# Two half-steps of a fused attention loop trade places

## The chip, the cores and the metric

The kernel runs on one core of a Trainium2 chip. The time is that of the whole launch on the device, in microseconds; lower is better. The core has a matrix engine (TensorE, shown as PE, its weight loads as PEld), a vector engine (VectorE, DVE), an engine for activation functions (ScalarE, ACT), a general engine (GpSimd, POOL), and queues that start DMA transfers. The engines run side by side and meet at semaphores. TensorE writes to PSUM, eight banks of 128 x 512 floats, from which VectorE and ScalarE read.

## What is computed

Two layers over an input of 2 images, 256 channels, 64 x 64 positions, all in fp32. The first layer is attention with 8 heads of 32 channels over 4096 positions, with a projection and a residual. The second is a non-local block (pooled keys and values, softmax over 1024 keys, a 1x1 convolution, batch normalization, residual). Nearly all time goes to the first:

```python
qkv = jnp.einsum('oc,bchw->bohw', w_qkv, x)
q, k, v = jnp.split(qkv, 3, axis=1)
...
scores = jnp.einsum('bhdi,bhdj->bhij', q, k) / jnp.sqrt(jnp.asarray(d, x.dtype))
attn = jax.nn.softmax(scores, axis=-1)
out = jnp.einsum('bhij,bhdj->bhdi', attn, v)
out = out.reshape(b, c, h, w)
return jnp.einsum('oc,bchw->bohw', w_proj, out) + x
```

## The kernel before

**Blocks and steps.** The attention of one image, one group of four heads (a quad) and 512 queries is a block: 2 images x 2 quads x 8 groups of queries make 32 blocks. A block (the class at L389, the loops at L529 to L569 in `attend`) takes its 4096 keys in 32 steps of 128; `j` counts them. A step needs, for each of the four heads, the scores of 128 keys against 512 queries (`score`, L404), their exponential (L551, two heads at a time, on ScalarE), and the sum of values weighted with them (`weigh`, L435), which is added to the running numerator `num` on VectorE (L450). The weighted sum of a step is issued one step later.

**Row groups.** A head has 32 channels, so a score matmul fills 32 of TensorE's 128 rows, and head h lies on rows 32h to 32h + 31. Matmuls on different rows can run at the same time. The weighted sum uses all 128 rows and 32 columns for each head.

**Maxima beside it.** The softmax subtracts the true maximum of each row. The maxima of a block are found a block earlier, in a second pass over the same scores, laid out with the queries on the partitions. That pass is a generator, `maxima` (L346), which `advance(maxes)` moves on by one half-step. Each half-step issues two products (`product`, L261), for two heads. So a step of the main loop has two slots, and in each the two score matmuls of one pair of heads stand beside two products of the other pair: four row groups in use.

**Plain and pair.** Heads 0 and 1 take their maxima plainly: each product of 512 keys goes to a VectorE reduce (`plain`, L273, the reduce at L276). Heads 2 and 3 take pairs of key chunks (`pair`, L278): a product with the difference of two chunks, whose relu ScalarE takes (L283), and in the next half-step of that head the product with the first chunk, to which VectorE adds the relu while it reduces (`joint`, L288; two instructions at L290). The two heads are a half-step apart, so each half-step of heads 2, 3 has one relu and one joint, the relu head first. In the first block of a new quad half of their work is plain too (L330). In the order before, the half-step of heads 2, 3 comes first in a step (L353), beside the scores of heads 0, 1 (L538), and that of heads 0, 1 second, beside the scores of heads 2, 3.

**The scores' banks.** Two tiles of two banks each hold the scores (`scores`, L68), one for each pair of heads, for four steps at a time. At `j % 4 == 0` the tile is started with the negative maxima (`subtract`, L424, two short matmuls; there the products are issued ahead of the scores), and in the next three steps the products with key differences are added to what stands there, so a score matmul waits for the exponential of the same pair one step before.

**The scratch banks.** The other four banks are one rotating pool, `ps_m` (L66, `scratch`, L71). The four products of a step, the weighted sum, and now and then a projection of q, k or v (`make`, L168), the row terms (`rows`, L147) or the denominator (L486) take a bank from it, in the order of issue; a new tile waits for whatever reads the tile that had the bank.

**Sums of the exponentials.** For the denominator, GpSimd adds the exponentials of heads 0, 1 into one tile (L469), and those of heads 2, 3 are added two steps at a time by accumulating DMA transfers, started from GpSimd's queue (L477) into two tiles that are added by one more such transfer (L483). The exponentials of heads 0, 1 lie in single tiles (six of them, L76), those of heads 2, 3 in double tiles for two steps (five, L79), which come free when their transfer has landed.

**Order.** Each engine runs its instructions in the order in which this code issues them, except that `issue_after` keeps an exponential behind the last relu issued (L549), and a few others behind named instructions. A step is: slot one, slot two, the weighted sum of the step before, the additions (`add`, L458), the pieces of normalization and projection that are due.

Of the kernel before, what the change touches and what calls it, by code (L numbers as in the profile page):

```python
# [35 lines left out]
def conv_attention(  # L36
# [31 lines left out]
    def scores(name):  # L68
        return ps_s.tile([P, 2, NB], F32, tag="s", name=name)
# [6 lines left out]
    def single(name):  # L76
        return probs.tile([P, 2, NB], F32, tag="one", name=name, bufs=ONES)

    def double(name):  # L79
        return probs.tile([P, 2, 2, NB], F32, tag="two", name=name, bufs=TWOS)  # L80
# [56 lines left out]
    def negate(name, neg):  # L137


        rest = work.tile([P, NB // P, QH], F32, tag="rest", name=f"rest_{name}")  # L140
        nc.gpsimd.tensor_copy(t[:, :, :, 0], neg)
        nc.gpsimd.tensor_sub(rest, neg, t[:, :, :, 0])
        nc.gpsimd.tensor_copy(t[:, :, :, 1], rest)
        nc.gpsimd.tensor_sub(rest, rest, t[:, :, :, 1])
        nc.gpsimd.tensor_copy(t[:, :, :, 2], rest)

        def rows():  # L147
            pt = scratch(f"pt_{name}")
            for j in range(NB // P):
                nc.tensor.matmul(  # L150
                    pt[:, bass.ts(j, P)],
                    t[:, j].rearrange("p h d -> p (h d)"),
                    ident_b,
                    start=True,
                    stop=True,
                )
            to = work.tile([P, NB], BF16, tag="rows", name=f"rows_{name}")
            nc.scalar.copy(to, pt)
            return to

        return rows
# [77 lines left out]
    def between(n, half):  # L239
        two = k[n][:, N // 2 * half + NB :]  # L240
        nc.gpsimd.tensor_sub(mid_kd[:, half, :], two[:, NB : 2 * NB], two[:, :NB])
# [3 lines left out]
    def during(n, i):  # L245
        if i < NI - 2:
            return [("q", n, i + 2), ("k", n + 1, i), ("v", n + 1, i)]
        if i == NI - 2:
            return [("k", n + 1, i), ("k", n + 1, i + 1), ("q", n + 1, 0)]
        return [("v", n + 1, i - 1), ("v", n + 1, i), ("q", n + 1, 1)]  # L250
# [50 lines left out]
    def first_block():  # L301


        for jp in range(NI // 2):
            for g in range(G):
                over = double(f"over_{jp}_{g}").rearrange("p a b n -> p (a b) n")
                for what in range(2):
                    if what == 0:
                        keys = (kd[0] if jp < NI // 4 else last_kd)[:, jp % (NI // 4), :]
                    else:  # L310
                        keys = k[0][:, bass.ts(2 * jp, NB)]
                    s = scores(f"ps_{jp}_{g}_{what}")
                    ps = [
                        product(0, 0, g, h, keys, s[:, h - 2, :] if h >= 2 else None)
                        for h in range(QH)
                    ]
                    for h in range(QH):
                        if what == 0:
                            nc.scalar.activation(over[:, h, :], ps[h], AF.Relu)
                        else:  # L320
                            joint(ps[h], over[:, h, :], g, h, jp)
                    yield
# [3 lines left out]
    def of_head(n, i, h):  # L326

        chunks = 0 if h < 2 else NI // 2 if i == 0 and n > 0 else NI  # L330
        pairs = [(g, jp) for jp in range(chunks // 2) for g in range(G)]
        plains = [(g, j) for g in range(G) for j in range(chunks, NI)]
        if h == 3:
            if not plains:
                g, jp = pairs.pop()
                plains = [(g, 2 * jp), (g, 2 * jp + 1)]
            plain(n, i, plains[0][0], h, plains[0][1])
            plains = plains[1:]
            yield
        for x in pairs:  # L340
            yield from pair(n, i, x[0], h, x[1])
        for x in plains:
            plain(n, i, x[0], h, x[1])
            yield

    def maxima(n, i):  # L346
        if (n, i) == (0, 0):
            yield from first_block()
        else:
            heads = [of_head(n, i, h) for h in range(QH)]  # L350
            for step in range(G * NI):

                for two in ((2, 3) if step % 2 == 0 else (3, 2)), (0, 1):  # L353
                    for h in two:
                        next(heads[h])
                    yield
        neg = work.tile([P, NB // P, QH], F32, tag="neg", name=f"neg_{n}_{i}")
        nc.vector.tensor_reduce(neg, part, AX.X, ALU.max, negate=True)
        rows.append(negate(f"{n}_{i}", neg))
        if i == 0 and n > 0:  # L360
            nc.vector.memset(part[:, :, 2:, :], LEAST)
# [11 lines left out]
    def advance(steps, n=1):  # L373
        for _ in range(n):
            next(steps, None)
# [12 lines left out]
    def attend(b, y):  # L388
# [15 lines left out]
        def score(s, pair, blk, j):  # L404

            half, c, cols = j // 16, j % 4, bass.ts(j % 16 // 4, P)
            if c == 0:
                kj = k[blk.n][:, bass.ts(keys(j), P)]
            elif c == 2:
                kj = mid_kd[:, half, cols]  # L410
            else:
                kj = (last_kd if half else kd[blk.n])[:, c // 2, cols]
            for t in range(2):
                h = 2 * pair + t
                nc.tensor.matmul(  # L415
                    s[:, t, :],
                    kj[bass.ts(h, D), :],
                    q[blk.n, blk.i][bass.ts(h, D), :],
                    start=False,
                    stop=True,  # L420
                    skip_group_check=j % 4 > 0,
                )

        def subtract(s, pair, blk):  # L424
            for t in range(2):
                h = 2 * pair + t
                nc.tensor.matmul(  # L427
                    s[:, t, :],
                    ones_b[bass.ts(h, D), :],
                    rows[blk.rows][bass.ts(h, D), :],  # L430
                    start=True,
                    stop=False,
                )
# [95 lines left out]
        for qd in range(QUADS):  # L529
            for i in range(NI):  # L530
                blk = Block(qd, i)
                items = [x for x in during(blk.n, i) if x[1] < len(QUAD)]
                both = [None, None]
                for j in range(NJ):
                    if j % 2 == 0:
                        two = double(f"p_{blk.name}_{j}_1")
                    p = [single(f"p_{blk.name}_{j}_0"), two[:, j % 2]]
                    for pair in range(2):  # L538
                        if j % 4 == 0:
                            s = both[pair] = scores(f"s_{blk.name}_{j}_{pair}")  # L540
                            subtract(s, pair, blk)
                            advance(maxes)
                            score(s, pair, blk, j)
                        else:
                            s = both[pair]
                            score(s, pair, blk, j)
                            advance(maxes)
                        with ExitStack() as order:
                            if cut is not None:  # L549
                                order.enter_context(tc.issue_after(cut.ins))  # L550
                            nc.scalar.activation(p[pair], s, AF.Exp, scale=scale)  # L551
                    if waiting is not None:
                        weigh(*waiting)
                        if j == 0:
                            normal = normalize(waiting[0])
                    add(blk, j, p, two)
                    waiting = blk, j, p
                    if j == 2 or j >= AFTER:
                        advance(normal)
                    if j % 2 == 0:  # L560
                        make_rows()
                        if (i, j) == (0, 2) and blk.n > 0:
                            between(blk.n, 1)
                        if (i, j) == (0, NJ // 4) and blk.n > 0:
                            differences(blk.n, 1, last_kd)
                        if (i, j) == (NI - 1, NJ // 2 + 2) and blk.n + 1 < len(QUAD):
                            between(blk.n + 1, 0)
                    elif j % 8 == 3 and j > 8 and items:
                        advance(make(*items.pop(0)), 9)  # L569
# [289 lines left out]
```

## Time and profile before

| | us |
|---|---|
| median of three runs | 4026.8 (4026.47 to 4027.5) |
| the profiled execution | 4027.6 |
| its span, first to last instruction | 4025.5 |
| until the first weighted sum | 103.5 |
| one block (630.00 to 735.65) | 105.65 |
| of it VectorE / ScalarE / GpSimd busy | 84.0 / 80.5 / 85.6 |
| projection and non-local layer, first image | about 292 |
| granted TensorE clock, mean | 0.997 |

The attention blocks take about 3.3 of the 4.0 ms, so what matters is the length of one step, 2.99 or 3.09 us, repeated some 600 times without anything else in it. TensorE shows busy throughout. Its records overlap: four matmuls on four row groups are in flight together, and an fp32 matmul is two passes, each with a record. On TensorE's timeline a step therefore shows as a row of starts 0.43 us apart, and its length is read from one weighted sum (L439) to the next. The timeline's columns are the start, the time covered by the group in us, the engine, line, operation and tiles, and in brackets the idle time before it with what ended it.

### The profile page before, as it was taken

To read this page: it belongs to the slowest core of one execution; us is meant where nothing else is said; L and a number is where in the kernel's file an instruction comes from. 1 tells how busy PE (TensorE), PEld (TensorE's weight loads), DVE (VectorE), ACT (ScalarE), POOL (GpSimd) and SP (SyncE) were. 2 spreads that over 40 slices of the span, in tenths; PEclk is the share of its full clock that TensorE was granted. 3 is DMA by queue.
4 is the path that set the end of the run, shared out by engine and by line. 5 is a ranking of instruction groups with operands and counts; after the bars stand their busy time and mean duration, and the time that the engine had idled before them with its cause. 6 is when DMAs were issued, how large, how long until landed. Compare 5 with 4: busy or idle time off the path is not lost.

```text
span 4025.5 us, 72980 instructions
## 1 busy us (share of the span) xinstructions
PE 3993.3 (99%) x28592; PEld 1460.0 (36%) x28592; DVE 2959.7 (74%) x5451; ACT 2668.1 (66%) x3328; POOL 2898.1 (72%) x1851
## 2 busy tenths in 40 slices
PE   9999999999999999999999999999999999999998
PEld 4333333333333333333333333333333333333333
DVE  5877777788777887774457877777888888884444
ACT  4777777777777777751137777777677777777121
POOL 1888888888888888871447888888888888886043
PEclk9999999999999999999999999999999999999999
DMA  1677777877777777880017787877788777778200
GB/s 56 141 163 159 161 165 162 168 162 165 159 161 163 161 161 162 169 199 12 21 35 163 163 167 164 167 161 167 161 167 166 162 162 163 162 161 184 72 16 26
DMA packets 113946, 569.60 MB, mean 141 GB/s; under 512 B 20296, under 2 KB 22600, under 8 KB 52416
## 3 DMA queue, kind: packets, MB, share of 16 engines
q0 software_dynamic: 68832, 501.25, 61.1%
q1 hardware_dynamic: 44080, 62.88, 5.3%
q8 instruction: 224, 3.67, 0.4%
q14 instruction: 122, 1.00, 0.1%
q10 hardware_dynamic: 688, 0.79, 0.1%
HBM read 54.78 MB, written 8.88 MB: 16 GB/s over the span
## 4 chain that ended last, share of the span: by engine, by line
PE 97%; DVE 2%; ACT 0%; POOL 0%; DMA 0%; issue 0%; DVEq 0%; ACTq 0%
PE ps L264 27%; PE w L439 25%; PE s L415 24%; PE y L715 5%; PE s L427 3%; PE v L186 2%; PE q L198 2%; PE k L198 2%; PE den L495 1%; PE proj L584 1%; PE g L640 1%; DVE r L729 1%; PE f L683 1%; PE f L749 1%; PE tp L624 0%; PE tp L620 0%
## 5 line engine op out<-in xcount | busy, mean ns | idle before, releaser
L469 POOL TENSOR_TENSOR p<-p,p 128x1024 f32<-128x1024 f32 x945 | 2293.6, 2427 | 569.9 <-ACT p L551 442.6
L264 PE MATMUL ps<-k,q 32*128 32x512 f32 x6232 | 2115.5, 619 | 2.4 <-DVE part L290 1.0
L551 ACT ACTIVATE p<-s 128x1024 f32<-128x1024 f32 x2048 | 1983.4, 1024 | 106.5 <-PE ps L264 61.2
L276 DVE TENSOR_REDUCE part<-ps 128x1 f32<-128x512 f32 x2136 | 1373.7, 686 | 87.9 <-PE ps L264 57.7
L290 DVE CUSTOM_DVE_ANT_0 ps<-ps,over 128x512 f32<-128x512 f32 x980 | 683.7, 700 | 572.3 <-PE ps L264 410.1
L439 PE MATMUL w<-p,v 128*32 128x512 f32 x8192 | 1092.7, 605 | 0.0
L283 ACT ACTIVATE over<-ps 128x512 f32<-128x512 f32 x916 | 547.2, 597 | 568.6 <-PE ps L264 552.0
L264 PEld LDWEIGHTS ps<-k,q 32*128 32x128 f32 x6232 | 809.7, 184 | 207.6 <-DVE part L276 48.6
L450 DVE TENSOR_TENSOR num<-num,w 128x512 f32<-128x512 f32 x992 | 670.7, 676 | 38.5 <-PE w L439 34.4
L264 PE MATMUL ps<-kd,q 32*128 32x512 f32 x1056 | 568.4, 643 | 1.0 <-POOL kd L219 0.7
L415 PE MATMUL s<-q,k 32*128 32x512 f32 x2048 | 514.6, 593 | 0.0
L415 PE MATMUL s<-q,last_kd 32*128 32x512 f32 x2048 | 510.1, 614 | 0.0
L415 PE MATMUL s<-q,kd 32*128 32x512 f32 x2048 | 509.9, 615 | 0.1
L415 PE MATMUL s<-q,mid_kd 32*128 32x512 f32 x2048 | 509.6, 615 | 0.0
L264 PE MATMUL ps<-last_kd,q 32*128 32x512 f32 x904 | 481.1, 639 | 1.5 <-POOL last_kd L219 1.5
L439 PEld LDWEIGHTS w<-p,v 128*32 128x32 f32 x8192 | 161.5, 108 | 777.4 <-ACT over L283 684.9
L477 POOL DMA_DIRECT2D p<-p x448 | 390.3, 871 | 66.0 <-ACT p L551 65.2
L415 PEld LDWEIGHTS s<-q,mid_kd 32*128 32x128 f32 x2048 | 173.5, 183 | 309.3 <-ACT p L551 306.8
L415 PEld LDWEIGHTS s<-q,kd 32*128 32x128 f32 x2048 | 174.2, 184 | 241.0 <-ACT p L551 215.1
L415 PEld LDWEIGHTS s<-q,last_kd 32*128 32x128 f32 x2048 | 173.5, 183 | 229.6 <-ACT p L551 213.0
L715 PE MATMUL y<-p,kv 128*128 128x512 f32 x512 | 240.0, 608 | 6.4 <-DVE r L729 6.4
L764 ACT ACTIVATE p<-f 128x1024 f32<-128x1024 f32 x64 | 65.5, 1024 | 248.5 <-PE f L749 219.2
(108 smaller groups left out, 2629.5 us busy)
## 6 DMA issues: line engine op xcount, KB each, us to landing
p<-p POOLq DMA_DIRECT2D x478, 1024.0 KB, 7.5
x_k<-in_x_dram SPq DMA_DIRECT2D x32, 512.0 KB
x_q<-in_x_dram SPq DMA_DIRECT2D x30, 512.0 KB
x_res<-in_x_dram SPq DMA_DIRECT2D x16, 512.0 KB
out_dram<-z SPq DMA_DIRECT2D x16, 512.0 KB
r<-flat SPq DMA_DIRECT2D x120, 64.0 KB
x_v<-in_x_dram SPq DMA_DIRECT2D x6, 512.0 KB
wqk_sb<-in_wqk_dram ACTq DMA_DIRECT2D x1, 512.0 KB
```

The source lines that it names most:

```text
L198: nc.tensor.matmul(pq, wqk_sb[:, c, qd, 0 if what == "q" else 1, :], xc[:, c, :], start=(c == 0), stop=(c == NC - 1),)
L264: nc.tensor.matmul(ps, q[n, i][bass.ts(h, D), bass.ts(g, P)], keys[bass.ts(h, D), :], start=True, stop=True,)
L276: reduced = nc.vector.tensor_reduce(part[:, g, h, j : j + 1], ps, AX.X, ALU.max)
L283: cut = nc.scalar.activation(over, ps, AF.Relu)
L290: reduced = nc.vector.tensor_tensor_reduce(out=ps, in0=ps, in1=over, scale=1.0, scalar=LEAST, op0=ALU.add, op1=ALU.max, accum_out=part[:, ...
L415: nc.tensor.matmul(s[:, t, :], kj[bass.ts(h, D), :], q[blk.n, blk.i][bass.ts(h, D), :], start=False, stop=True, skip_group_check=j % 4 > 0,)
L439: nc.tensor.matmul(w[bass.ts(h, D), :], v[blk.n][:, keys(j), h, :], p[h // 2][:, h % 2, :], start=True, stop=True,)
L450: nc.vector.tensor_add(blk.num, blk.num, w)
L469: added = nc.gpsimd.tensor_add(blk.sums[0], blk.sums[0], p[0])
L477: nc.gpsimd.dma_start(out=blk.sums[n], in_=two, accum_op=ALU.add)
L551: nc.scalar.activation(p[pair], s, AF.Exp, scale=scale)
L715: nc.tensor.matmul(acc[i][o], wg[:, 2 * t + j, bass.ts(o, P)], p[:, j, :], **edge)
```

## The change

The two slots of a step trade places: the scores of heads 2, 3 beside the plain products of heads 0, 1 come first, and the scores of heads 0, 1 beside the pair products of heads 2, 3 second. The weighted sum stays at the end of the step, and which scores stand beside which products stays too.

```diff
             for step in range(G * NI):
 
-                for two in ((2, 3) if step % 2 == 0 else (3, 2)), (0, 1):
+                for two in (0, 1), ((2, 3) if step % 2 == 0 else (3, 2)):
                     for h in two:
                         next(heads[h])
                     yield
...
                     p = [single(f"p_{blk.name}_{j}_0"), two[:, j % 2]]
-                    for pair in range(2):
+                    for pair in (1, 0):
                         if j % 4 == 0:
                             s = both[pair] = scores(f"s_{blk.name}_{j}_{pair}")
                             subtract(s, pair, blk)
```

## The prediction

> **What bounds the kernel now.** I read the page's busy shares first, then its chain, then the table of waits, and then the timeline of one stretch, since shares hide which wait ends last.
>
> ```profile
> PE 3993.3 (99%) x28592; PEld 1460.0 (36%) x28592; DVE 2959.7 (74%) x5451; ACT 2668.1 (66%) x3328; POOL 2898.1 (72%) x1851
> PE 97%; DVE 2%; ACT 0%; POOL 0%; DMA 0%; issue 0%; DVEq 0%; ACTq 0%
> ```
>
> TensorE is never empty, but a matmul counts as busy while it waits its turn in a row group, so 99% does not say that it runs at its own pace. The table of waits (total us, times, longest) shows who holds it:
>
> ```profile
> PEld s L415 <- ACT p L551: 735.0, 1104, 1.0
> PEld w L439 <- ACT over L283: 684.9, 903, 0.8
> ...
> PEld ps L264 <- DVE num L450: 41.8, 211, 0.4
> ```
>
> The two long rows are about 0.7 us each time, at every change between the scores' tiling and the weighted sum's tiling: the weight load waits for the array to empty, whatever engine is named. The third row is small, but it is the one that is late. TensorE's timeline (start, length, group):
>
> ```profile
> 1000.46 1.07 PE L439 MATMUL w<-p,v 128*32 128x512 f32 x8
> 1001.45 0.70 PE L415 MATMUL s<-q,last_kd 32*128 32x512 f32 x2
> ...
> 1002.84 0.59 PE L264 MATMUL ps<-k,q 32*128 32x512 f32 x1
> 1002.86 0.59 PE L415 MATMUL s<-q,last_kd 32*128 32x512 f32 x2
> 1002.93 0.59 PE L264 MATMUL ps<-k,q 32*128 32x512 f32 x1
> 1003.45 1.06 PE L439 MATMUL w<-p,v 128*32 128x512 f32 x8
> 1004.44 0.70 PE L415 MATMUL s<-q,mid_kd 32*128 32x512 f32 x2
> ...
> 1006.02 0.59 PE L264 MATMUL ps<-k,q 32*128 32x512 f32 x1
> 1006.53 1.07 PE L439 MATMUL w<-p,v 128*32 128x512 f32 x8
> 1007.53 0.70 PE L415 MATMUL s<-q,last_kd 32*128 32x512 f32 x2
> ```
>
> One step of 128 keys is first slot, second slot, weighted sum W. Step one lasts 1004.44 − 1001.45 = 2.99, the next 3.09. In the second one the last product stands alone at 1006.02, and W starts 0.52 later; in the first it is at 1002.93, some 0.06 behind its mates. The weight loads and VectorE say why:
>
> ```profile
> 1002.39 0.21 PEld L264 LDWEIGHTS ps<-k,q 32*128 32x128 f32 x2 [0.20 <-DVE num L450]
> ...
> 1005.48 0.29 PEld L264 LDWEIGHTS ps<-k,q 32*128 32x128 f32 x2
> ```
>
> ```profile
> 1002.82 0.70 DVE L290 CUSTOM_DVE_ANT_0 ps<-ps,over 128x512 f32<-128x512 f32 x1 [0.48 <-PE ps L264]
> 1003.44 0.14 DVE L290 DVE_READ_ACCUMULATOR2_ANT part<- 128x1 f32 x1
> 1003.55 1.29 DVE L276 TENSOR_REDUCE part<-ps 128x1 f32<-128x512 f32 x2
> 1004.75 0.68 DVE L450 TENSOR_TENSOR num<-num,w 128x512 f32<-128x512 f32 x1
> ```
>
> Per step five tiles go through four scratch banks in turn, so each waits for the tile four places earlier. Before, the order is relu head, joint head, plain, plain, W; the second plain product takes the bank of the last W, which the addition into num frees. That addition stands last in VectorE's queue, at 1004.75 to 1005.43; the load follows 0.05 later (1005.48). This closes a loop over two steps. From a first slot's start: joint +1.37, num ends +3.98, load +4.03, the late product's second pass +0.535 (1005.48 to 1006.02), W +0.52, next first slot +0.99: 6.08. Measured: 1007.53 − 1001.45 = 6.08.
>
> TensorE alone would need 0.96 (slot to slot) + 0.97 (second slot to W, its last pass on time) + 0.99 = 2.92 a step.
>
> **What the Trainium skill says.** "TensorE: Matmul & The Clock Gate", Part 3, The mechanism: matmuls in different row groups overlap, but start and end in program order. The trace agrees: four start within 0.02 us, and one late product holds W. "TensorEngine Tiling (Array Packing)", Key Properties: a change of tiling mode drains TensorE; the trace shows 0.99 from W's start to the next slot for two passes of 0.43. "PSUM — Partial Sum Buffer", Specifications: 8 banks of 2 KiB; here four hold the scores, four the scratch. The first page also calls ScalarE's and VectorE's queues strict FIFO (Part 1, Architectural detail), and in the timeline num never passes the reduces ahead of it.
>
> **The change part by part.** No instruction is added or removed. The order of the built program shows that the pairing stays (scores of heads 0, 1 beside products of heads 2, 3, and the reverse); only the place of W in the cycle moves. Let 0 be the start of the new first slot (plain products c, d), the pair products being a (relu) and b (joint).
>
> *Banks.* The order becomes c, d, a, b, W. So W waits for c's reduce of the same step, d for the relu a of the step before, b for the num addition. The waits in the built program name just these.
>
> *VectorE.* A slot's first results are complete 1.13 after its start, and an engine picks them up 0.08 later (relu 1002.67 after an end at 1002.59). c's reduce 1.21 to 1.90 (0.69); d 0.61 later, 1.82; joint 0.61 later, 2.43 (its data is there at 0.96 + 1.37 = 2.33); num 0.72 after the joint (1002.82 to about 1003.54), 3.15, since W's data comes at about 3.10; it ends at 3.83. Before it was 3.98: the joint no longer leads the queue with VectorE idle before it. Then load 3.88, second pass +0.535 = 4.41, W 4.93, next slot 5.92 for two steps, 0.16 less than 6.08.
>
> *New wait.* c's reduce ends at 1.90, release 0.05: W may start at 1.95, where TensorE alone gives 1.93. So a step is at least 1.95 + 0.99 = 2.95.
>
> *Sum.* Every fourth step has the row subtraction and is TensorE's own (3.13 between W starts; about 3.12 after). The three between take 2.99, 3.09, 2.985 = 9.06 before; after, 2.95, 5.92 − 2.95 = 2.97, 2.95 = 8.87. Over the block from 630.00 to 735.65 (105.65 us, 32 steps) 21 steps have neither subtraction, projection, row terms nor denominator; W to W they sum to 63.5, mean 3.025. After: 21 × 2.957 = 62.1, so 1.4 us a block. Maxima run beside blocks 0 to 30; in three of them (842.1 to 950.7 is one, 108.6 us) half the steps have four plain reduces, VectorE-bound in either order, so I count 29.5: 29.5 × 1.4 = 41 us.
>
> *Cost at nothing, and its cover.* ScalarE now runs exp of heads 2, 3, relu, exp of heads 0, 1. First exp 1.22; relu 2.12 (0.905 behind it); other exp 2.62 to 3.64, release 3.69, its scores' second pass 4.23, needed at 4.32: 0.09 spare. Without that cover each 0.1 costs 0.1. The relu frees d's bank at 2.77, needed at 2.95. GpSimd's addition of p[0] moves 0.9 later and its DMA start goes ahead of the odd addition; two additions and one DMA start take about 5.6 us (998.10, 1001.15, less idle) against 5.9 for two steps. The exp of heads 2, 3 comes 1.4 earlier and at step 6 waits for the DMA at L483 (6.9 from issue to landing), issued 0.9 later: before there were 3.0 us between landing and exp, now 0.6. If that is missed, the denominator's matmuls of the same step (1.65 us) cover it. Startup, projection and the non-local layer are not touched.
>
> The profiled execution took 4027.6 (span 4025.5 and 2.1 around it), 0.8 above the median. 4026.8 − 41 = 3986.
>
> **The rivals.**
> *No change:* W is a load across a change of tiling, and no wait of that kind decides in the trace. I took 0.05, as for num; if the release there costs 0.12 instead, or the joint takes a little more behind a busy VectorE, a step grows to 3.02 and the gain is gone: 4020 to 4035. For it: W then stands on a same-step loop without slack. Against: c's reduce starts on an idle VectorE, num having ended at 3.83 − 2.95 = 0.88.
> *Slower:* c's reduce comes too late for W. Place: W's weight load; it decides from 0.07 beyond my 1.95, where a step passes 3.025. Each further 0.1 costs 0.1 × 21 × 29.5 = 62 us. If c runs 0.2 late (num of the step before still on VectorE at 1.4), W is at 2.15, a step 3.14, and the time 4026.8 + 0.115 × 620 = 4098; at half that 4060. Against: num must end 0.5 later than worked out.
> *Larger gain:* the reduce is not late after all and a step is 2.92: 0.1 × 620 = 62 us, 3965. The lowest common distance before is 2.93 to 2.95.
> *That nothing moves:* excluded by the built order.
>
> **How the numbers follow.** Main case 0.66 (3968 to 4005, from 0.03 us a step either way: 0.03 × 620 = 19), larger gain 0.09, no real change or a remnant of gain 0.14 (half of it within 0.2%, about 8 us, which is what a measurement tells from no change), slower 0.11. The range 3964 to 4024 leaves out most of the slower case and part of the third. Faster by over 0.2%: 0.66 + 0.09 + 0.06 = 0.81; within: 0.08; slower: 0.11.
>
> **What would show it.** W-to-W distances of plain steps of 2.95 to 2.98 in place of 2.99 and 3.09; num ending 3.83 after a first slot's start; PEld w named as waiting for DVE part L276 in place of ACT over L283; blocks of about 104.2 us. Wrong would be: num still at 3.98, W over 1.02 behind the second slot's start, or steps of heads 0, 1 whose second pass waits for ScalarE.

## The result and the profile after

The changed kernel takes 3987.0 us (median of five, 3985.0 to 3990.4) against 4026.8: ratio 0.9901, 95% interval 0.9888 to 0.9914. The forecast was 3986. The profiled execution took 3986.4 us, span 3984.6, against 4027.6 and 4025.5.

The first page of the profile after, busy shares and chain by engine:

```profile
PE 3949.7 (99%) x28592; PEld 1450.9 (36%) x28592; DVE 2937.8 (74%) x5451; ACT 2671.5 (67%) x3328; POOL 2903.6 (73%) x1851
PE 97%; DVE 2%; DMA 0%; ACT 0%; POOL 0%; issue 0%; DVEq 0%; ACTq 0%
```

By shares nothing has happened, although 41 us are gone. The table of waits (total us, times, longest) has changed hands:

```profile
PEld w L439 <- DVE part L276: 769.4, 986, 1.5
...
PEld s L415 <- ACT over L283: 539.2, 643, 0.8
```

The weighted sum's loads now name VectorE's plain reduce. Most of the 769 us is again the emptying of the array, about 0.76 each time; the part that matters is the few hundredths beyond it. The wait for num has shrunk from 41.8 to 8.7 us, as the group of the products' weight loads shows (after the bar: idle time and what ended it):

```profile
L264 PEld LDWEIGHTS ps<-k,q 32*128 32x128 f32 x6232 | 636.5, 183 | 55.7 <-DVE num L450 8.7
```

One plain step of the kernel after, with the start of the step ahead of it, TensorE's timeline (start, length, group):

```profile
989.92 0.70 PE L415 MATMUL s<-q,last_kd 32*128 32x512 f32 x2
...
991.89 1.07 PE L439 MATMUL w<-p,v 128*32 128x512 f32 x8
992.88 0.70 PE L415 MATMUL s<-q,mid_kd 32*128 32x512 f32 x2
...
993.43 0.59 PE L264 MATMUL ps<-k,q 32*128 32x512 f32 x2
...
994.27 0.59 PE L264 MATMUL ps<-last_kd,q 32*128 32x512 f32 x1
...
994.30 0.59 PE L264 MATMUL ps<-k,q 32*128 32x512 f32 x1
994.85 1.06 PE L439 MATMUL w<-p,v 128*32 128x512 f32 x8
995.84 0.70 PE L415 MATMUL s<-q,last_kd 32*128 32x512 f32 x2
```

The last product no longer trails: the last passes of the second slot start within 0.03 of each other, 994.27 to 994.30. But W starts 0.55 after the last of them instead of 0.52. The step is 995.84 − 992.88 = 2.96. The weight loads and VectorE over the same step:

```profile
993.76 0.18 PEld L264 LDWEIGHTS ps<-k,q 32*128 32x128 f32 x1
...
994.85 0.16 PEld L439 LDWEIGHTS w<-p,v 128*32 128x32 f32 x8 [0.79 <-DVE part L276]
```

```profile
992.35 0.69 DVE L290 CUSTOM_DVE_ANT_0 ps<-ps,over 128x512 f32<-128x512 f32 x1
...
993.02 0.69 DVE L450 TENSOR_TENSOR num<-num,w 128x512 f32<-128x512 f32 x1
994.10 1.29 DVE L276 TENSOR_REDUCE part<-ps 128x1 f32<-128x512 f32 x2 [0.39 <-PE ps L264]
```

num ends at 993.71 and the pair product takes its bank at 993.76, in time for its slot. VectorE then stands idle for 0.39, starts head 0's reduce at 994.10, 1.22 after the slot's start, and ends it 0.69 later at 994.79; W's load follows at 994.85. That is the new wait of the forecast.

Plain steps are those without subtraction, projection, row terms or denominator. From W to W, 583 of the 705 now take 2.96, where 2.99, 3.09 and 2.985 took turns; longer ones are left mainly at the start of a block (3.22, then 3.00) and in the blocks with four plain reduces. The usual block went from 105.65 to 104.25 us. From the first to the last matmul of the weighted sums the time fell by 40.4 us (3628.9 to 3588.5).

### The profile page after: what moved, and what is told of

Read it like the earlier page. It is cut to its first block, busy times and chain, and to the rows that moved or that the text cites. A ratio compares the mean times of both kernels' runs of the same rounds, so it can differ in the third digit from the quotient of the medians.

```text
span 3984.6 us, 72269 instructions
## 1 busy us (share of the span) xinstructions
PE 3949.7 (99%) x28592; PEld 1450.9 (36%) x28592; DVE 2937.8 (74%) x5451; ACT 2671.5 (67%) x3328; POOL 2903.6 (73%) x1851
## 4 chain that ended last, share of the span: by engine, by line
PE 97%; DVE 2%; DMA 0%; ACT 0%; POOL 0%; issue 0%; DVEq 0%; ACTq 0%
PE w L439 26%; PE ps L264 26%; PE s L415 24%; PE y L715 6%; PE s L427 3%; PE q L198 2%; PE v L186 2%; PE k L198 2%; PE den L495 1%; PE g L640 1%; DVE r L729 1%; PE f L683 1%; PE proj L584 1%; PE f L749 1%; PE tp L624 0%; PE tp L620 0%
## 5 line engine op out<-in xcount | busy, mean ns | idle before, releaser
L469 POOL TENSOR_TENSOR p<-p,p 128x1024 f32<-128x1024 f32 x945 | 2324.7, 2460 | 557.0 <-ACT p L551 550.1
L551 ACT ACTIVATE p<-s 128x1024 f32<-128x1024 f32 x2048 | 2089.9, 1025 | 624.1 <-PE ps L264 408.5
L264 PE MATMUL ps<-k,q 32*128 32x512 f32 x6232 | 2049.0, 627 | 4.0 <-DVE part L276 1.7
L450 DVE TENSOR_TENSOR num<-num,w 128x512 f32<-128x512 f32 x992 | 681.4, 687 | 92.7 <-PE w L439 91.3
L264 PEld LDWEIGHTS ps<-k,q 32*128 32x128 f32 x6232 | 636.5, 183 | 55.7 <-DVE num L450 8.7
L264 PE MATMUL ps<-kd,q 32*128 32x512 f32 x1056 | 518.2, 595 | 0.7 <-POOL kd L219 0.7
L264 PE MATMUL ps<-last_kd,q 32*128 32x512 f32 x904 | 437.4, 590 | 1.5 <-POOL last_kd L219 1.5
```

What stands on the lines that cost most here:

```text
L264: nc.tensor.matmul(ps, q[n, i][bass.ts(h, D), bass.ts(g, P)], keys[bass.ts(h, D), :], start=True, stop=True,)
L450: nc.vector.tensor_add(blk.num, blk.num, w)
L469: added = nc.gpsimd.tensor_add(blk.sums[0], blk.sums[0], p[0])
```

## The experiments

The theory: before, plain steps were bound by a loop over two steps, in which the num addition frees the bank of the next second plain product; after, by a loop within a step, in which head 0's reduce frees the bank of the weighted sum. The rivals: the exponentials' new order on ScalarE or GpSimd's new order made the gain; VectorE's load as such counts; the place of the products alone counts.

**Half of the num addition, before and after.** The addition into num takes 256 of 512 columns; half of the numerator is left unadded.

```diff
-                nc.vector.tensor_add(blk.num, blk.num, w)
+                nc.vector.tensor_add(blk.num[:, : NB // 2], blk.num[:, : NB // 2], w[:, : NB // 2])
```

> The kernel before, but the addition into num (L450) takes only 256 of the 512 columns, so half of the numerator is left unadded; every instruction and wait stays, and the addition is some 0.27 us shorter. Bank theory (before is bound over two steps by num, which frees the bank of the second plain product): the loop of 6.08 us falls to 5.81, under TensorE's own 5.85; plain steps go from 2.99/3.09 to about 2.93, 62 us less, and some 6 us more in the blocks with four plain reduces: about 3958. Rival (the exponentials' place on ScalarE, or the place of GpSimd's work, made the difference): ScalarE and GpSimd are untouched, so 4015 to 4027.

> The same edit on the changed kernel: half of the numerator is left unadded. Bank theory: plain steps are now set by the reduce of head 0, which frees the bank of the weighted sum, and num is off the path: plain steps stay at 2.96, and only the blocks with four plain reduces gain: about 3980. Rival (num still bounds it, or VectorE's load as a whole): 0.1 or more a step, 3920 to 3930.

Measured 3963.9 (ratio 0.9843, 0.9828 to 0.9857) on the kernel before, 3977.9 (0.9877, 0.9862 to 0.9892) on the changed one. The same saving on VectorE is worth 63 us before and 9 after. VectorE's num in the cut kernel before, and TensorE's W starts around it:

```profile
1003.96 0.41 DVE L450 TENSOR_TENSOR num<-num,w 128x256 f32<-128x256 f32 x1
```

```profile
1002.60 1.06 PE L439 MATMUL w<-p,v 128*32 128x512 f32 x8
...
1005.52 1.06 PE L439 MATMUL w<-p,v 128*32 128x512 f32 x8
```

num is 0.27 shorter, and its plain steps fall to 2.92 or 2.93 (the distance shown is 2.92), with none at 3.09. This is the pace that the prediction worked out for TensorE alone, and no run here has a lower one; the loop that ends with num was what held the kernel before. After, plain steps stay at 2.96 (W at 1001.74 and 1004.70, for instance). The 9 us come mostly from the blocks with four plain reduces (108.1 to 106.2), the rest from a subtraction step in six late blocks (3.84 to 3.57) and the second step of a block (3.00 to 2.96).

**Half of one plain reduce, after.** Head 0 in one run, head 1 in the other; its maxima miss half of the keys. One line is added, so later lines stand one further.

```diff
-        reduced = nc.vector.tensor_reduce(part[:, g, h, j : j + 1], ps, AX.X, ALU.max)
+        few = ps[:, : NB // 2] if h == 0 else ps
+        reduced = nc.vector.tensor_reduce(part[:, g, h, j : j + 1], few, AX.X, ALU.max)
```

> The changed kernel, the plain reduce of head 0 over 256 of 512 columns, so its maxima miss half of the keys. Bank theory: the weighted sum no longer waits for that reduce; plain steps fall from 2.96 to TensorE's own 2.92 or 2.93, 0.03 x 620 = about 20 us less, and about 6 in the blocks with four plain reduces: about 3960. Rival (2.96 is TensorE's own pace, the wait is only named last): about 3981.

> The changed kernel, the plain reduce of head 1 (in place of head 0) over 256 of 512 columns, so its maxima miss half of the keys. VectorE has exactly the same work as in the run with head 0 cut. Bank theory: head 0's reduce still frees the weighted sum's bank at the same moment, plain steps stay at 2.96, about 3980. Rival (VectorE's total load counts): as with head 0, about 3960.

Measured 3962.1 (0.9839, 0.9823 to 0.9856) with head 0 cut, 3977.9 (0.9878, 0.9863 to 0.9893) with head 1 cut. VectorE saves the same in both; what counts is which reduce. TensorE's W starts with head 0 cut, and with head 1 cut (second fence):

```profile
1002.07 1.06 PE L440 MATMUL w<-p,v 128*32 128x512 f32 x8
...
1004.99 1.07 PE L440 MATMUL w<-p,v 128*32 128x512 f32 x8
```

```profile
1001.49 1.07 PE L440 MATMUL w<-p,v 128*32 128x512 f32 x8
...
1004.45 1.07 PE L440 MATMUL w<-p,v 128*32 128x512 f32 x8
```

That is 2.92 here (2.93 in most plain steps), against 2.96 with head 1 cut. In the plain steps, then, head 0's reduce holds W after the change, and VectorE's total load doesn't. The 9 us that the cut of head 1 still gains lie mostly in the blocks with four plain reduces, as with num (108.1 to 106.2).

**One half of the change alone.** Only L353 is changed; the scores keep their order.

```diff
-                for two in ((2, 3) if step % 2 == 0 else (3, 2)), (0, 1):
+                for two in (0, 1), ((2, 3) if step % 2 == 0 else (3, 2)):
```

> One half of the change alone: the maxima's half-steps trade places (L353) and the scores do not, so in each slot the scores and the products are of the same two heads. Row-group theory: four passes of 0.43 us follow each other on each of two row groups while the other two are empty for part of the slot; a step gets 0.5 to 0.9 us longer, 4500 to 4900. Rival (the places of the maxima alone made the gain, and what stands beside them doesn't matter): about 3987.

Measured 4742.3, in one run. TensorE's timeline of this kernel, scores and products of a first slot:

```profile
1504.98 1.13 PE L415 MATMUL s<-q,last_kd 32*128 32x512 f32 x4
1505.94 0.59 PE L264 MATMUL ps<-k,q 32*128 32x512 f32 x2
```

The first slot's scores start at 1504.98, its products, on the same rows, at 1505.94 where they would otherwise start 0.02 after. Plain steps are mostly 3.76. This edit alone loses 716 us, so the place of the products alone did not make the gain. The other half alone, which would pair the same rows, was not run.

**The weighted sum between the slots.** The slots stand as before; the weighted sum is issued between them, two steps late.

```diff
-                    if waiting is not None:
-                        weigh(*waiting)
-                        if j == 0:
-                            normal = normalize(waiting[0])
...
+                        if pair == 0 and len(waiting) == 2:
+                            old = waiting.pop(0)
+                            weigh(*old)
+                            if j == 1:
+                                normal = normalize(old[0])
```

> The slots as in the kernel before (pairs of heads 2, 3 first), but the weighted sum is issued between the two slots instead of after them, and two steps late instead of one. In a cycle this is the order of the changed kernel: plain products, pair products, weighted sum. Bank theory: the plain steps take 2.96 and the time is that of the changed kernel, 3980 to 3995. Rival (what counts is which exponential comes first in a step and when GpSimd's additions and DMAs are issued, which here stand as before): 4015 to 4030.

Measured 4073.8 (1.0115, 1.0100 to 1.0130): the forecast of the time failed. Plain steps are 2.96 as the theory has them, so the loss is elsewhere, and my edit had made it. The block took 107.33 instead of 104.25. The largest piece is the step ahead of a block's first weighted sum, 4.17 us, where TensorE's weight loads wait for GpSimd:

```profile
1181.93 0.16 PEld L439 LDWEIGHTS w<-p,v 128*32 128x32 f32 x8 [2.00 <-POOL p L469]
```

The second step's exponentials are added in place into the tile of the first (`blk.sums[0]`), so the late weighted sum of heads 0, 1 had to wait for that addition, and read its result: that part of the computation is changed. The rest is row terms (4.01 for 3.29), denominators and projections, which no longer stand behind a weighted sum, and 0.08 for each subtraction. So I moved what follows the weighted sum along with it, the additions of the step before included:

```diff
+                        if pair == 1:
+                            continue
+                        if len(waiting) == 2:
+                            old = waiting.pop(0)
+                            weigh(*old)
+                            if j == 1:
+                                normal = normalize(old[0])
+                        if fresh is not None:
+                            add(*fresh)
...
+                    fresh = blk, j, p, two
```

> The slots in the order of the kernel before. Between the two slots stand the weighted sum of two steps ago and, behind it, the additions of the step before, normalization, row terms and projections, so that the cycle is plain products, pair products, weighted sum, the rest, as in the changed kernel; within a step the exponential of heads 0, 1 is still the first and GpSimd's two additions still stand ahead of the DMA start. The subtraction's matmuls fall on both sides of a weighted sum, which cost 0.08 a subtraction in the run with the weighted sum alone moved: 0.08 x 8 x 31 = 20. Bank theory: plain steps 2.96 and the rest as in the changed kernel, 3985 to 4010. Rival (exponentials' order within a step, GpSimd's order): 4020 or more, plain steps of 2.99 and 3.09.

Measured 4003.1 (0.9941, 0.9924 to 0.9957), plain steps 2.96, the usual block 105.0. TensorE's W starts:

```profile
1009.98 1.07 PE L439 MATMUL w<-p,v 128*32 128x512 f32 x8
...
1012.94 1.07 PE L439 MATMUL w<-p,v 128*32 128x512 f32 x8
```

The slots' order within a step, the first exponential and GpSimd's order are those of before, and more than half of the gain is there; what is missing, some 16 us, fits the 0.08 of each subtraction (3.14 + 3.03 for the pair of steps against 3.13 + 2.96). What counts is the cycle: plain products, pair products, weighted sum.

**Products ahead of the scores in the first slot**, on the changed kernel:

```diff
                             advance(maxes)
                             score(s, pair, blk, j)
+                        elif pair == 1:
+                            s = both[pair]
+                            advance(maxes)
+                            score(s, pair, blk, j)
                         else:
                             s = both[pair]
```

> The changed kernel with the plain products issued ahead of the scores in every first slot (not only where the negative maxima are subtracted), nothing left out. Bank theory: head 0's product ends 0.014 us earlier (two places of 0.007), so its reduce and with it the weighted sum start 0.014 earlier: plain steps 2.945, 0.014 x 620 = 9 us less, about 3978. Rival (VectorE takes the tile up at a fixed time or the scores' later end counts): 3985 to 3990.

Measured 3972.5 (0.9862, 0.9847 to 0.9877), a larger gain than expected; plain steps 2.93. TensorE's and VectorE's timelines:

```profile
1197.00 0.70 PE L264 MATMUL ps<-k,q 32*128 32x512 f32 x2
...
1197.53 0.59 PE L264 MATMUL ps<-k,q 32*128 32x512 f32 x2
```

```profile
1198.16 1.29 DVE L276 TENSOR_REDUCE part<-ps 128x1 f32<-128x512 f32 x2 [0.34 <-PE s L415]
```

The reduce starts 1.16 after the slot's start instead of 1.22. The expected 0.014 is there, but VectorE also takes the tile up 0.04 after the product's end (1197.53 + 0.59) instead of 0.08 (993.43 + 0.59 to 994.10). With 0.06 off, W is free of the reduce and TensorE's own pace is reached. The last section shows where the 0.04 between the two comes from.

**More work on ScalarE**, on the changed kernel: the relu is taken again over 128 columns, which leaves the values as they are.

```diff
-        cut = nc.scalar.activation(over, ps, AF.Relu)
+        nc.scalar.activation(over, ps, AF.Relu)
+        cut = nc.scalar.activation(over[:, :128], over[:, :128], AF.Relu)
```

> The changed kernel with the relu taken a second time over 128 of its 512 columns, in place (same values): one more ScalarE instruction of 0.2 to 0.3 us in each pair half-step, between the first relu and the exponential of heads 0, 1. Theory (ScalarE has cover): in the changed kernel the exponential ends 3.61 after a first slot's start and may end at 3.82 before its scores hold the weighted sum, so up to 0.2 more costs nothing and 0.3 costs about 0.05 a step: 3984 to 4020. Rival (the exponentials' place on ScalarE is what the change gained from, and ScalarE is on the path): the whole 0.2 to 0.3 in each of about 900 steps, 4170 to 4260.

Measured 4087.9 (1.0150, 1.0133 to 1.0167), between the two. ScalarE's timeline of one step, and that of the changed kernel without the addition (second fence):

```profile
1194.44 0.60 ACT L283 ACTIVATE over<-ps 128x512 f32<-128x512 f32 x1
1195.07 0.31 ACT L284 ACTIVATE over<-over 128x128 f32<-128x128 f32 x1
1195.29 1.01 ACT L552 ACTIVATE p<-s 128x1024 f32<-128x1024 f32 x1
```

```profile
994.98 0.59 ACT L283 ACTIVATE over<-ps 128x512 f32<-128x512 f32 x1
995.47 1.02 ACT L551 ACTIVATE p<-s 128x1024 f32<-128x1024 f32 x1
```

From relu to exponential it is 0.85 instead of 0.49: 0.36 more, not 0.2 to 0.3. About half of the plain steps (343 of 705) take 3.12; most of the others lie between 2.96 and 3.06. I had reckoned with a loop over two steps, so with half the cost; it is within one: the exponential frees the scores of heads 0, 1, the pair products stand behind those scores in TensorE's queue, and the next relu needs them: 0.05 + 0.535 + 0.59 + 0.08 + 0.85 + 1.02 = 3.12. Without the addition that sum is 2.76, so ScalarE has 0.2 in hand against the step of 2.96, and a step at 3.12 pays in full for what goes beyond it. That it has a cover was right, its form was not.

**The step behind ScalarE's copy**, added to products first: a block's first weighted sum is copied into num by VectorE.

```diff
-                nc.scalar.copy(blk.num, w)
+                nc.vector.tensor_copy(blk.num, w)
```

> The changed kernel with the plain products ahead of the scores in the first slot, and the first weighted sum of a block copied into num by VectorE instead of ScalarE (L448). In the run with products first the step after that copy takes 3.34 us, since the bank of the weighted sum comes free only when ScalarE has done both exponentials. By VectorE the copy stands where the addition stands in other steps. Bank theory: that step falls to about 2.93, 0.41 x 31 = 13 us less, about 3960. Rival (another wait holds that step, or VectorE falls behind): 3970 or more.

Measured 3961.0 (0.9837, 0.9822 to 0.9851). The step fell from 3.34 to 3.02, not quite to 2.93, and the next one from 3.00 to 2.93. This kernel leaves nothing out and is the fastest complete kernel of the study.

## Why the prediction was right

- **What bounds it.** The bank loop of 6.08 over two steps was read correctly: cutting only num brings the kernel before to TensorE's pace.
- **VectorE's part.** num was to end at 3.83 from a first slot's start and ended at 3.79 (993.71 − 989.92): it follows the joint 0.67 behind instead of 0.72 (992.35 to 993.02).
- **The new wait.** W was to start at 1.95 and starts at 1.97, since the reduce begins at 1.22 instead of 1.21 and the release takes 0.06 instead of 0.05. So plain steps are 2.96 where I had 2.95, 2.97, 2.95: the mean the same to 0.003 us. The two steps at 2.95 were too short, and the middle one had the wrong bound: I still had num setting it (5.92 for two steps), but num, ending at 3.79, would allow 3.79 + 0.05 + 0.535 + 0.52 + 0.99 = 5.885, less than two steps of 2.96, and the run with num cut on the changed kernel shows it off the path. That the errors cancel is luck; the new wait, which sets the pace, was forecast to 0.02.
- **The sum.** 1.4 us a block was forecast and 1.40 came; in the blocks with four plain reduces, counted at half, 0.5. The total of 41 stands against 39.8 between medians.
- **Cost at nothing.** It held. The transfer at L483 now lands 0.34 us ahead of the exponential that waits for it (median of 30 blocks), against 3.0 before and the 0.6 forecast; in some blocks the exponential waits, but the denominator's step, 4.64 before, is 4.68, no more than the reduce explains. ScalarE's cover, 0.09 in the forecast, is about 0.2 by the run with more relu.
- **The rivals.** No change would have needed a release of 0.12; it is 0.06. The slower case needed head 0's reduce to find VectorE busy; VectorE stands idle for 0.39 ahead of it. The larger gain was 2.92 a step: the wait of 0.03 denies it, and the runs with head 0 cut and with products first show that it was no more than that wait.

## What to carry to other kernels

With more tiles than banks in a rotating pool, write down which tile takes whose bank and compare each release with the moment it is needed; the loop that is late by hundredths of a microsecond sets the pace, though its wait is among the smallest in the table. A cyclic shift of the work can match early releases to early needs without removing an instruction. Then look for the one instruction that closes the loop: cutting its length, or a neighbour's of equal length, tells in two runs whether it is the release or the engine's load.

## What was not expected of the hardware

VectorE took up head 0's product 0.04 us after its end, as the profile gives it, when it was the first of the four matmuls in flight, and 0.08 when it was the third. The changed kernel shows both by itself: in its steps with a subtraction, where the products stand ahead of the scores, the delay is 0.04 (987.33 + 0.59 to 987.96).

The traces also record the semaphore increments by which an engine tells that it is done. In the plain step shown above, the first slot has three: one for the pair of scores, then one for each product. These matmuls end 0.007 apart, but the increments come at 994.034, 994.077 and 994.119, so 0.043 and 0.042 apart, and VectorE starts 0.023 behind the second. With products first, head 0's increment stands first, at 1198.134, and VectorE starts 0.023 behind it. So the 0.04 is the one increment that stood ahead. The Trainium skill, "TensorE: Matmul & The Clock Gate", Part 3, The cost: per-tile semaphore tail, says that such increments come one after another, about 26 ns each. The traces agree that they come one after another, but here they are 42 or 43 ns apart. In a loop that is late by 0.03 the position within a group of parallel matmuls was worth 14 us.
